# Layer 0's experts of a decoder: every expert for every row, against blocks of rows sorted by expert

## Chip, core and metric

The kernel runs on one core of one Trainium2 chip, as one program with one launch. The metric is the device time of an execution in microseconds (us). The kernel before has a median of 3429.14 us in three runs, which lie between 3427.95 and 3429.79 us.

## What is computed

The input x has 32 sequences of 100 tokens and 256 features (3200 rows), and there is a context of 361 rows for each sequence. Two layers follow each other. Each consists of a self-attention, a cross-attention on the context, and a feed-forward part with eight experts. The change is in layer 0's feed-forward part:

```
x1 = layer_norm(x + attention(x)) * ln1_w + ln1_b
gates = softmax(x1 @ gate_w.T + gate_b)             # 8 experts
_, top_idx = top_k(gates, 2)
expert_outputs = einsum('bsd,efd->bsef', x1, expert_w) + expert_b
moe_out = sum over the two chosen e of gates[e] * expert_outputs[e]
out = layer_norm(x1 + moe_out) * ln2_w + ln2_b      # then x = x + out
```

Each row needs two of eight 256x256 matrices. All arithmetic is in fp32.

## The kernel before

The 32 sequences are worked through in eight groups of four (NG = 8, G = 4, so a group has GT = 400 rows). A function `heads_attention` makes the self-attention with one loop over sequences; one turn of it is called a step here. The order of TensorE, VectorE, ScalarE and GpSimd in the loop is the order in which the program writes the calls (`in_order`). In each step the scores of the next sequence are made (line L363), masked and reduced to a maximum on VectorE (L372, L383), lowered by it on GpSimd (L384) and put through the exponential on ScalarE (L389). The weights of the present sequence are turned (L396, L401) and multiplied with the values (L412), and the sequence before is divided (L425, L432), turned (L438) and multiplied with the output matrix (the product with `f_wo`, in line L225 of the helper `project`). At four places of each step the loop calls `fill(s, part)`, which puts other work between.

In layer 0's feed-forward part `fill` holds the gating and the experts of groups that the attention has already left. `rows_of` adds the output bias on GpSimd (L1235) and normalises the rows; `gating` turns them, makes the gate logits and the two largest gates; `gates_turned` (L1293) turns the gates of a group and stores them to DRAM. From there `gate` (L1311) loads the gates of one expert, repeated over all partitions. `gated` (L1321, VectorE) multiplies the group's rows by the gates of one expert, which are zero where the expert wasn't chosen. `experts` (L1328, L1333) multiplies the gated rows of every expert with its matrix, a pair of experts in each step, after a small product that adds the biases; VectorE adds the pairs up (L1339). `end` turns the sum back (L1359), normalises it, and GpSimd multiplies, shifts and adds it to x (L1371 to L1373). After the 32 sequences the loop goes on for nine more steps, in which only the last experts, some constants and the first projections of the next self-attention (`project_group`) are left.

The next stage is layer 1's self-attention. Its loop has 16 numbers for each group: `first` (L1467) makes small products that ScalarE puts through tanh (L1473), `second` (L1486) multiplies those, and a table `around` says at which number the next group's projections stand. One of them, part 9, makes a small tile `own` on GpSimd (L1199), which part 10 multiplies on TensorE. SyncE's queue carries the DMAs; where it isn't in the set of `in_order`, a scheduler places them. In layer 1's feed-forward part, which isn't changed, rows are already sorted by expert: GpSimd sends rows with an indirect DMA (L1759), SyncE loads a place into a register and fetches a block of 128 rows from there (L2131), its matrix in the same way (L2122), and results are added into DRAM with an indirect DMA (L2352). TensorE loads the expert's number into a register after two transposes of the block (L2315).

Of the kernel before, what the change touches and what calls it, by code (L numbers as in the profile page):

```python
# [10 lines left out]
F32 = mybir.dt.float32  # L11
# [7 lines left out]
P = 128  # L19
# [47 lines left out]
def kernel(ctx: ExitStack, tc: tile.TileContext, io: dict, out: bass.AP):  # L67
# [40 lines left out]
    causal = early.tile([T, T], F32, name="causal")  # L108

# [117 lines left out]
    def in_order(more=mybir.EngineType.Pool):  # L227

        e = mybir.EngineType
        return tc.manual_schedule(engines={e.PE, e.DVE, e.Activation, more})  # L230
# [50 lines left out]
    def heads_attention(pool, w, wo, bias, norm, turn, res, fill, ready=0, over=None):  # L281
# [172 lines left out]
        with in_order():  # L454
# [17 lines left out]
            for s in range(B + 1 + fill.steps):  # L472
# [44 lines left out]
                if s == B and over:  # L517
                    over()
# [112 lines left out]
    with tc.tile_pool(name="a0", bufs=2) as pool:  # L631
# [69 lines left out]
        fill.steps = 0  # L701
# [354 lines left out]
    def top2(pool, val, n, iota8, np_=T):  # L1056
# [9 lines left out]
        for k in range(2):  # L1066
            nc.vector.tensor_tensor(
                hot[:np_, k, :n, :], bc(iota8[:np_], 1, n),
                idf[:np_, :n, k : k + 1].to_broadcast([np_, n, 8]), ALU.is_equal,
            )  # L1070
        return top, hot
# [140 lines left out]
    attn = attn_cm.__enter__()  # L1212
    with tc.tile_pool(name="f0x", bufs=1) as fixed, tc.tile_pool(name="f0", bufs=2) as pool:
        f0_we = weight(fixed, "f0_we", D, E * D)
        f0_eb = plain(fixed, "f0_eb", [E, D])
# [10 lines left out]
        x1s, x1Ts, wts, accs = {}, {}, {}, {}  # L1226

        parts = {}
        wt_dram = dram.tile([NG, E * GT], F32, name="wt_dram")

        def rows_of(g, part):

            xl = xls[g]
            if part == 0:
                nc.gpsimd.tensor_tensor(xl, xl, bc(row("f0_bo"), 1, G), ALU.add)  # L1235
            elif part == 1:
                parts[g] = stats(xl, G, tag="r", shift=True)
            else:
                x1 = pool.tile([T, G, D], F32, tag="x1", name="x1")
                scaled(x1, xl, G, parts[g])  # L1240
                x1s[g] = x1
                xls.pop(g)

        def gating(g, part):
            if part == 0:
                x1T = pool.tile([P, 2, GT], F32, tag="x1T", name="x1T")
                transposed(x1T, x1s.pop(g), "f0_ln1w", "f0_ln1b", tiles=mm_tile)
                x1Ts[g] = x1T
                return
            if part == 1:  # L1250
                x1T = x1Ts[g]
# [25 lines left out]
            lg = parts.pop(g)  # L1277
            sm = small.tile([T, G], F32, tag="smg", name="smg")
            nc.vector.tensor_reduce(sm, lg, AX.X, ALU.add)
            nc.vector.reciprocal(sm, sm)  # L1280
            gt = small.tile([T, G, E], F32, tag="gt", name="gt")
            nc.vector.tensor_tensor(gt, lg, bc(sm, 2, E), ALU.mult)
            _, hot = top2(pool, gt, G, row("iota", P))
            wt = small.tile([T, G, E], F32, tag="wt", name="wt")
            nc.vector.tensor_tensor(wt, hot[:T, 0], hot[:T, 1], ALU.add)
            nc.vector.tensor_tensor(wt, wt, gt, ALU.mult)
            wts[g] = [wt]

        def gates_turned(g):
            wt = wts[g][0]  # L1290
            pw = mm_tile()
            for i in range(G):
                nc.tensor.matmul(  # L1293
                    pw[:E, i * T : (i + 1) * T], wt[:, i, :], ident[:T, :T],
                    start=True, stop=True,
                )
            wtT = small.tile([E, GT], F32, tag="wtT", name="wtT", bufs=2)
            evac(wtT, pw[:E, :GT])
            nc.sync.dma_start(wt_dram[g].rearrange("(e t) -> e t", e=E), wtT)
            wts[g] = wtT  # L1300

        wbs, xgs = {}, {}

        def gate(n):

            if n < E * NG:
                g, e = n // E, n % E
                wb = pool.tile([P, GT], F32, tag="wb", name="wb", bufs=3)  # L1310
                nc.sync.dma_start(  # L1311
                    wb, wt_dram[g : g + 1, e * GT : (e + 1) * GT].to_broadcast([P, GT])
                )
                wbs[n] = wb

        def gated(n):
            if n < E * NG:

                tag = "xg" if n < 2 * (B - 2 * G) else ("xg", "xlT", "xrT")[(n // 2 + 1) % 3]
                xg = (pool if tag == "xg" else ahead).tile([P, 2, GT], F32, tag=tag, name="xg")  # L1320
                nc.vector.tensor_tensor(xg, x1Ts[n // E], bc(wbs.pop(n), 1, 2), ALU.mult)  # L1321
                xgs[n] = xg

        def experts(g, i, m):
            ps = mm_tile()
            at = slice(m * P, (m + 1) * P)
            if i == 0:
                nc.tensor.matmul(ps[:, :GT], f0_eb[:, at], wts[g], start=True, stop=False)  # L1328
                if m == 0:
                    accs[g] = pool.tile([P, 2, GT], F32, tag="acc", name="acc", bufs=1)  # L1330
            for e in range(2 * i, 2 * i + 2):
                for k in range(2):
                    nc.tensor.matmul(  # L1333
                        ps[:, :GT], f0_we[:, k, e * D + m * P : e * D + (m + 1) * P],
                        xgs[E * g + e][:, k, :], start=(i > 0 and e == 2 * i and k == 0),
                        stop=(e == 2 * i + 1 and k == 1),
                    )
            acc = accs[g][:, m, :]
            nc.vector.tensor_tensor(  # L1339
                acc, ps[:, :GT], x1Ts[g][:, m, :] if i == 0 else acc, ALU.add  # L1340
            )
            if m == 1:
                xgs.pop(E * g + 2 * i), xgs.pop(E * g + 2 * i + 1)

        def end(g, part):
            if part == 0:

                yo = (pool if g < NG - 1 else next_cms[0][1]).tile(
                    [T, G, D], F32, tag="x1" if g < NG - 1 else "yo", name="yo",
                    bufs=2 if g < NG - 1 else 1,  # L1350
                )
                acc = accs.pop(g)
                x1Ts.pop(g)
                for i2 in range(2):
                    pt = mm_tile()
                    for i in range(2):
                        for c in range(2):
                            tok = slice((2 * i2 + i) * T, (2 * i2 + i + 1) * T)
                            nc.tensor.transpose(  # L1359
                                pt[:T, i * D + c * P : i * D + (c + 1) * P], acc[:, c, tok], ident  # L1360
                            )
                    nc.scalar.copy(
                        yo[:, 2 * i2 : 2 * i2 + 2, :].rearrange("p g d -> p (g d)"), pt[:T, :]
                    )
                x1s[g, "end"] = yo
            elif part == 1:
# [1136 lines left out]
```

## Time and profile before

| | us |
|---|---|
| median of three runs | 3429.14 |
| the profiled execution | 3428.13 |
| its span, first to last instruction | 3426.4 |
| first product with layer 0's expert matrices (L1333) | 839.5 |
| last product with f_wo in layer 0's feed-forward part | 1189.5 |
| first product of layer 1's self-attention (L1467) | 1267.4 |
| first product of layer 1's cross-attention (x_wq) | 1609.0 |

The mean granted clock of TensorE was 0.985 of full speed. The profile counts an engine as busy from the start of an instruction to its end, and overlapping instructions once. PE is TensorE's matmuls and PEld its weight loads, DVE is VectorE, ACT is ScalarE, POOL is GpSimd, SP is SyncE; "SPq" marks an instruction of SyncE's queue. A matmul in fp32 is recorded as two instructions, a transpose as one. Each group of instructions is shown as line, engine, operation, tile written and tiles read, shapes and count, then busy us and the mean ns of one, then the idle time of its engine just before and who ended it.

### The profile page before, as it was taken

The page shows a single profiled execution, that of the slowest core. Times are in us where ns is not written, and L with a number is a line of the kernel's source. Part 1 is how long each engine was busy: PE and PEld are TensorE (multiplying, and loading weights), DVE is VectorE, ACT ScalarE, POOL GpSimd, SP SyncE. Part 2 cuts the span into 40 slices and gives each one's busy share as a digit, 9 for nine tenths or more (in the row PEclk, how much of TensorE's full clock was granted, in tenths as well). Part 3 has the DMA queues.
Part 4 walks back from the last instruction along what each step waited for, and adds up shares of the span by engine and source line. Part 5 has one row for each costly group of instructions (what it writes and reads, how often), then busy time and mean ns, then how long its engine had stood idle before and what let it go on. Part 6 is the DMA issues. An engine that isn't in the chain of part 4 may idle for free. (4 is left out here: it accounts for less than half of the span.)

```text
span 3426.4 us, 65400 instructions
## 1 busy us (share of the span) xinstructions
PE 3288.5 (96%) x25492; PEld 2217.0 (65%) x25492; DVE 1807.2 (53%) x5122; ACT 1630.8 (48%) x3597; POOL 1246.3 (36%) x936
## 2 busy tenths in 40 slices
PE   8998999989999989999999999999999989999997
PEld 6775666656666543333666666666666658899997
DVE  5776666658776658563546555564655441011111
ACT  4665666756444326665545555454555532211111
POOL 3435888854344330011323333333343332022221
PEclk8999999999999999999999999999999999999999
DMA  3002211110010120001000000000000013456665
GB/s 91 2 15 60 53 52 52 35 41 19 26 30 25 40 68 1 1 1 39 10 17 17 24 28 27 15 28 23 17 28 19 21 44 116 153 168 186 185 182 140
DMA packets 116316, 179.86 MB, mean 52 GB/s; under 512 B 16594, under 2 KB 95194, under 8 KB 115546
## 3 DMA queue, kind: packets, MB, share of 16 engines
q1 hardware_dynamic: 101340, 157.37, 14.8%
q0 software_dynamic: 12688, 15.36, 2.5%
q8 instruction: 204, 3.34, 0.4%
q10 hardware_dynamic: 1982, 2.95, 0.3%
q14 instruction: 102, 0.84, 0.1%
HBM read 150.09 MB, written 28.82 MB: 52 GB/s over the span
## 5 line engine op out<-in xcount | busy, mean ns | idle before, releaser
L1907 POOL TENSOR_TENSOR ex<-ex,rc 100x1444 f32<-100x1444 f32 x128 | 331.6, 2591 | 770.0 <-DVE rc L1906 525.8
L1898 ACT ACTIVATE ex<-s,nmx 100x361 f32<-100x361 f32 x512 | 303.2, 594 | 121.2 <-DVE nmx L1889 121.2
L384 POOL TENSOR_TENSOR s<-s,nmx 100x800 f32<-100x800 f32 x128 | 195.3, 1526 | 305.7 <-DVE nmx L383 217.7
L1473 ACT ACTIVATE h<-sc,cols 128x800 f32<-128x800 f32 x256 | 222.1, 923 | 101.4 <-PE sc L1467 99.9
L1889 DVE CUSTOM_DVE_ANT_0 s<-sc,mb 100x361 f32<-100x361 f32 x512 | 250.4, 527 | 7.5 <-PE sc L1882 7.5
L2352 POOL DMA_INDIRECT acc_dram<-y,xg x57 | 89.5, 1570 | 447.6 <-DVE y L2351 259.6
L2334 ACT ACTIVATE hgT<-sc 128x1024 f32<-128x1024 f32 x57 | 58.3, 1023 | 351.2 <-PE sc L225 351.2
L225 PE MATMUL sc<-xgT,w1b 128*128 128x128 f32 x1824 | 213.1, 275 | 0.4 <-DMA w1b<-in_f_w 0.4
L2351 DVE TENSOR_SCALAR y<-mm,gx 128x256 f32<-128x256 f32 x57 | 27.6, 484 | 347.9 <-PE mm L225 347.9
L225 PEld LDWEIGHTS sc<-xgT,w1b 128*128 128x128 f32 x1824 | 208.2, 192 | 0.7 <-issue 0.6
L225 PE MATMUL mm<-wx,hgT 128*128 x912 | 206.1, 379 | 0.0
L1333 PE MATMUL mm<-xg,f_we 128*128 128x400 f32 x512 | 191.3, 515 | 14.2 <-DVE xg L1321 13.7
L1882 PE MATMUL sc<-kT,qT 64*100 64x361 f32 x1024 | 197.6, 463 | 0.0
L1854 PE MATMUL mm<-x_wa,cT 128*128 128x512 f32 (+1 forms) x512 | 188.6, 491 | 0.2
L225 PEld LDWEIGHTS mm<-wx,hgT 128*128 128x128 f32 x912 | 169.0, 190 | 20.6
L1824 PE MATMUL mm<-cT,x_wa 128*128 128x361 f32 x512 | 179.7, 470 | 1.1 <-ACT lnT L139 1.1
L1932 PEld LDWEIGHTS mm<-eT,vb 128*64 128x64 f32 (+1 forms) x3072 | 136.6, 137 | 67.3 <-issue 66.4
L1914 PE MATMUL mm<-ident,ex 100*128 100x100 f32 (+1 forms) x1536 | 166.5, 257 | 10.1 <-ACT kT L1836 5.3
L1921 ACT COPY eT<-mm 128x400 f32<-128x400 f32 (+1 forms) x256 | 125.6, 491 | 100.2 <-PE mm L1914 99.6
L1932 PE MATMUL mm<-eT,vb 128*64 128x100 f32 (+1 forms) x3072 | 161.9, 254 | 0.0
L1914 PEld LDWEIGHTS mm<-ident,ex 100*128 100x128 f32 (+1 forms) x1536 | 143.1, 152 | 28.7 <-ACT kT L1836 7.4
L176 POOL TENSOR_TENSOR rs<-va,neghalf 100x4 f32<-100x4 f32 (+1 forms) x95 | 94.6, 998 | 178.7 <-DVE va L172 89.5
(370 smaller groups left out, 7064.7 us busy)
## 6 DMA issues: line engine op xcount, KB each, us to landing
w1b<-in_f_w SPq DMA_DIRECT2D x57, 1024.0 KB
wb<-wt_dram SPq DMA_DIRECT2D x64, 200.0 KB
cT<-in_ctxT SPq DMA_DIRECT2D x64, 180.5 KB
cT<-in_ctxT SPq DMA_DIRECT2D x128, 90.2 KB
wx<-in_f_w SPq DMA_DIRECT2D x8, 1024.0 KB
xg<-sorted_dram SPq DMA_DIRECT2D x57, 132.5 KB
cb<-in_ctx SPq DMA_DIRECT2D x32, 192.0 KB
x_dram<-x SPq DMA_DIRECT2D x32, 100.0 KB
```

The source lines that it names most:

```text
L225: nc.tensor.matmul(ps, lhsT[k], rhs[k], start=(k == 0), stop=(k == n - 1))
L384: nc.gpsimd.tensor_tensor(sm, sm, bc(nmx, 2, T), ALU.add)
L1333: nc.tensor.matmul(ps[:, :GT], f0_we[:, k, e * D + m * P : e * D + (m + 1) * P], xgs[E * g + e][:, k, :], start=(i > 0 and e == 2 * i and ...
L1473: nc.scalar.activation(h1, both[r2][:, :, :GT], AF.Tanh, bias=col("a1_b1", o))
L1824: nc.tensor.matmul(kTs[u][c][:, :S2], x1_wa[:, m * P : (m + 1) * P], cT[:, 0, :], start=True, stop=False,)
L1854: nc.tensor.matmul(ps[e][:kn, :n], cT[:, 0, at], x1_wa[:, 1024 + c0 : 1024 + c0 + n], start=True, stop=False,)
L1882: nc.tensor.matmul(ps[:T, e, :S2], qT[p0 : p0 + 64, m, tok], kT[p0 : p0 + 64, c, :], start=True, stop=True,)
L1889: nc.vector.tensor_tensor_reduce(s[:, e, :], ps[:T, e, :S2], mb, 1.0, 3.4e38, ALU.add, ALU.min, nmx[:, e : e + 1],)
L1898: nc.scalar.activation(ex[:, 2 * c + e, :], s[:, e, :], AF.Exp, bias=nmx[:, e : e + 1], scale=-1.0, accum_out=sm[:, 2 * c + e : 2 * c + e ...
L1907: nc.gpsimd.tensor_tensor(ex, ex, bc(rc, 2, S2), ALU.mult)
L1914: nc.tensor.transpose(pt[:kn, j * T : (j + 1) * T], ex[:, j, k0 : k0 + kn], ident[:T, :T])
L1932: nc.tensor.matmul(po[64 * e : 64 * e + 64, m * T : (m + 1) * T], vb[k][:kn, v0 + 64 * h : v0 + 64 * h + 64] if k < 2 else vb[2 + u % 2][: ...
```

## The change

Layer 0's experts are no longer multiplied for every row. The first four groups and the last four each get a list in DRAM, in which the rows are sorted by expert. The changes are these:

- `gating` makes for each row and each of its two experts the place in the list, from counts that two small products with a triangular matrix give. `gates_turned`, `gate`, `gated`, `experts` and `end` go.
- `send0` writes the normalised rows of a sequence to both places with two indirect DMAs on GpSimd. A small memset stands before each. `rest` fills the block behind the end of each expert's rows with zeros, and 14 stores fill spare blocks at the start. `table` makes on VectorE which expert and which place each block of 128 rows has.
- The layer norm's gain and shift and the experts' biases are folded into the matrices (`expert_bias`, `expert_weights`), in the first eight steps. The normalised rows themselves are also stored, in order, for the later sum.
- The attention loop ends with its 33rd step. Then a loop over 64 blocks (MOST = 32 in each list) follows: fetch the block, turn it, multiply it with one matrix, store the result in DRAM. SyncE's and GpSimd's order is the program's here too. Group 7's gating, the lists of the second half, group 0 and 1's endings and the first projections of the next stage stand in this loop.
- The end of a group is now: load the stored rows, apply gain and shift on GpSimd, gather the two results of each row with two indirect DMAs a sequence, add them weighed on VectorE, normalise, scale on ScalarE, multiply, shift and add. For groups 2 to 7 this stands in the loop of layer 1's self-attention (`later`).
- The bias of the attention's output is added for one sequence at a time, and the statistics of a group are made in two halves.

The core of the diff:

```diff
+    SOME, MOST = -(-2 * PART // P), (2 * PART + E * 127) // P
+    EMPTY = MOST - SOME
...
+    def rows_back(g):
+        rt = next_cms[1][1].tile([T, G, D], F32, tag="rt", name="rt")
+        nc.sync.dma_start(rt.rearrange("p g d -> p (g d)"), x1_dram[g])
+        x1back[g] = rt
+    def rows_affine(g):
+        rt = x1back[g]
+        for k, op in enumerate((ALU.mult, ALU.add)):
+            nc.gpsimd.tensor_tensor(rt, rt, bc(constants["ln1"][:, k, :], 1, G), op)
+    def outputs_back(g, i):
+        yb = next_cms[1][1].tile([T, 2, D], F32, tag="yb", name="yb", bufs=4)
+        for k in range(2):
+            nc.gpsimd.indirect_dma_start(
+                yb[:, k, :], None, y_dram[g // HALF][:, :],
+                bass.IndirectOffsetOnAxis(ap=from0[:, k, g * G + i : g * G + i + 1], axis=0),
+            )
+        ysback[g, i] = yb
+    def weighed(g, i):
+        yb = ysback.pop((g, i))
+        xi = x1back[g][:, i, :]
+        for k in range(2):
+            nc.vector.scalar_tensor_tensor(
+                xi, yb[:, k, :], gates0[:, g * G + i, k : k + 1], xi, ALU.mult, ALU.add
+            )
+    def second_norm(g, half_):
+        last_sums[g] = stats(
+            x1back[g], G, tag="e", shift=True, half=half_, got=last_sums.get(g)
+        )
+    def second_scaled(g):
+        scaled(x1back[g], x1back[g], G, last_sums.pop(g))
+    def second_added(g, engine, two=slice(0, G)):
+        rt, n = x1back[g][:, two], two.stop - two.start
+        engine.tensor_tensor(rt, rt, bc(row("f0_ln2w"), 1, n), ALU.mult)
+        engine.tensor_tensor(rt, rt, bc(row("f0_ln2b"), 1, n), ALU.add)
+        engine.tensor_tensor(xs[g][:, two], xs[g][:, two], rt, ALU.add)
...
+        for p in range(2):
+            for t in range(EMPTY):
+                at = E * RGP + t * P
+                nc.sync.dma_start(rows_dram[p][at : at + P, :], zero)
...
+        def expert_bias(e):
+            eb = biases[e] = pool.tile([P, D], F32, tag="xg", name="eb", bufs=6)
+            nc.sync.dma_start(eb, io["f0_eb"][e : e + 1].to_broadcast([P, D]))
+        def expert_weights(e, part):
+            eb = biases[e]
+            if part == 0:
+                ps = mm_tile()
+                project(
+                    ps[:, :D], [shift[:, c, :] for c in range(2)], [we[:, c, e, :] for c in range(2)]
+                )
+                nc.vector.scalar_tensor_tensor(
+                    eb, eb, 1.0 / D, ps[:, :D], ALU.mult, ALU.add
+                )
+                return
+            gain = cols[:, COL_AT["f0_ln1w"][0] : COL_AT["f0_ln1w"][1]]
+            nc.gpsimd.tensor_tensor(we[:, :, e, :], we[:, :, e, :], bc(gain, 2, D), ALU.mult)
+            nc.gpsimd.tensor_tensor(we[:, :, e, :], we[:, :, e, :], bc(eb, 1, 2), ALU.add)
+            biases.pop(e)
...
+        def send0(g, i):
+            b = g * G + i
+            for k in range(2):
+                nc.gpsimd.memset(pace, 0.0)
+                unordered(
+                    nc.gpsimd.indirect_dma_start(
+                        rows_dram[g // HALF][:, :],
+                        bass.IndirectOffsetOnAxis(ap=pos0[:, k, b : b + 1], axis=0),
+                        x1s[g][:, i, :], None,
+                    ), f"puts{g // HALF}", puts[g // HALF],
+                )
+            if i == G - 1:
+                x1s.pop(g)
...
+        def rest(p, e):
+            at = nc.sync.value_load(rest0[p][0:1, e : e + 1], min_val=0, max_val=E * RGP - P)
+            unordered(
+                nc.sync.dma_start(rows_dram[p][bass.ds(at, P), :], zero), f"puts{p}", puts[p]
+            )
...
+        def fetch(n):
+            if n >= 2 * MOST:
+                return
+            p, t = n // MOST, n % MOST
+            at = nc.sync.value_load(
+                rows_at[p][0:1, t : t + 1], min_val=0, max_val=E * RGP + (EMPTY - 1) * P
+            )
+            xg = xgs[n] = pool.tile([P, D], F32, tag="xg", name="xg", bufs=6)
+            after(nc.sync.dma_start(xg, rows_dram[p][bass.ds(at, P), :]), puts[p])
+        def turned0(n):
+            if n >= 2 * MOST:
+                return
+            p, t = n // MOST, n % MOST
+            xg = xgs.pop(n)
+            pt = mm_tile()
+            for c in range(2):
+                nc.tensor.transpose(
+                    pt[:, c * P : (c + 1) * P], xg[:, c * P : (c + 1) * P], ident
+                )
+            xT = pool.tile([P, 2, P], F32, tag="xgT", name="xgT")
+            nc.vector.tensor_scalar_add(
+                xT.rearrange("p c t -> p (c t)"), pt[:, : 2 * P], 1.0
+            )
+            xgTs[n] = xT
+            experts_[n] = nc.tensor.value_load(
+                expert_of[p][0:1, t : t + 1], min_val=0, max_val=E - 1
+            )
+        def product(n):
+            xT, e = xgTs.pop(n), experts_.pop(n)
+            po = mm_tile()
+            project(
+                po[:, :D], [xT[:, c, :] for c in range(2)],
+                [we[:, c, bass.ds(e, 1), :] for c in range(2)],
+            )
+            y = pool.tile([P, D], F32, tag="y", name="y", bufs=3)
+            nc.scalar.copy(y, po[:, :D])
+            nc.sync.dma_start(y_dram[n // MOST][n % MOST * P : n % MOST * P + P, :], y)
...
+        def after_group(g, at):
+            return {
+                3: ((output_bias, G * g + 3),), 4: ((rows_of, g, 1),), 6: ((rows_of, g, 2),),
+                8: ((gating, g, 0),), 9: ((gating, g, 1),), 10: ((gating, g, 2),),
+                11: ((gating, g, 3),), 13: ((gating, g, 4),), 14: ((gating, g, 5),),
+                15: ((send0, g, 0),), 19: ((send0, g, 1),), 23: ((send0, g, 2),),
+                27: ((send0, g, 3),),
+            }.get(at, ())
...
+        with in_order(pool_, sp_):
+            g = NG - 1
+            todo = {
+                0: ((send0, g - 1, 2), (rows_of, g, 1), (send0, g - 1, 3)), 3: ((rows_of, g, 2),), 5: ((gating, g, 0),),
+                6: ((gating, g, 1),), 8: ((gating, g, 2),), 9: ((gating, g, 3),),
+                11: ((gating, g, 4),), 12: ((gating, g, 5),),
+                13: (*((send0, g, i) for i in range(G)), (table, 1, 0)),
+                14: (*((rest, 1, e) for e in range(E)), (table, 1, 1)), 15: ((table, 1, 2),), 17: ((table, 1, 3), (table, 1, 4)),
+                16: ((make_constants, 0),), 18: ((make_constants, 1),), 20: ((make_constants, 2),),
+                21: ((rows_back, 0), (rows_affine, 0)), 23: ((rows_back, 1), (rows_affine, 1)),
+                MOST + 1: tuple((outputs_back, 0, i) for i in range(G)),
+                MOST + 5: ((weighed, 0, 0),), MOST + 7: ((weighed, 0, 1),),
+                MOST + 8: ((second_norm, 0, 0),),
+                MOST + 9: ((weighed, 0, 2),), MOST + 10: ((weighed, 0, 3),),
+                MOST + 11: ((second_norm, 0, 1), (outputs_back, 1, 0), (outputs_back, 1, 1)),
+                MOST + 14: ((second_scaled, 0),),
+                MOST + 15: ((second_added, 0, nc.vector, slice(0, 2)), (outputs_back, 1, 2)),
+                MOST + 16: ((second_added, 0, nc.vector, slice(2, 4)), (outputs_back, 1, 3)),
+                MOST + 17: ((project_group, 0, 0),), MOST + 18: ((weighed, 1, 0),),
+                MOST + 20: ((project_group, 0, 1),),
+                MOST + 21: ((weighed, 1, 1), (project_group, 0, 2)),
+                MOST + 22: ((project_group, 0, 3),), MOST + 23: ((weighed, 1, 2),),
+                MOST + 24: ((project_group, 0, 4), (weighed, 1, 3)),
+                MOST + 25: ((project_group, 0, 5), (second_norm, 1, 0)),
+                MOST + 26: ((project_group, 0, 6),),
+                MOST + 27: ((project_group, 0, 7), (second_norm, 1, 1)),
+                MOST + 28: ((project_group, 0, 8),),
+                MOST + 29: ((project_group, 0, 9), (second_scaled, 1)),
+                MOST + 30: ((project_group, 0, 10), (second_added, 1, nc.gpsimd)),
+            }
+            for n in range(4):
+                fetch(n)
+            turned0(0)
+            for n in range(2 * MOST):
+                fetch(n + 4)
+                turned0(n + 1)
+                product(n)
+                for f, *args in todo.get(n, ()):
+                    f(*args)
...
+    later = {
+        0: ((rows_back,), (outputs_back, 0), (outputs_back, 1)), 2: ((rows_affine,),),
+        3: ((outputs_back, 2),), 4: ((outputs_back, 3),), 5: ((weighed, 0),), 6: ((weighed, 1),),
+        7: ((second_norm, 0),), 8: ((weighed, 2),), 9: ((weighed, 3),), 10: ((second_norm, 1),),
+        12: ((second_scaled,),), 13: ((second_added, nc.gpsimd),),
+    }
```

## Prediction

> **What bounds the kernel now.** I read the page first, for which engine is full.
>
> ```profile
> PE 3288.5 (96%) x25492; PEld 2217.0 (65%) x25492; DVE 1807.2 (53%) x5122; ACT 1630.8 (48%) x3597; POOL 1246.3 (36%) x936
> PE   8998999989999989999999999999999989999997
> ```
>
> TensorE is the bound in nearly every slice, so work taken from it counts wherever nothing else becomes the limit. The changed stage starts near 745 us. The groups of instructions between 740 and 1300 us (busy us, mean ns, idle before) price what goes and what moves:
>
> ```profile
> L1333 PE MATMUL mm<-xg,f_we 128*128 128x400 f32 x512 | 191.3, 515 | 14.2 <-DVE xg L1321 13.7
> L384 POOL TENSOR_TENSOR s<-s,nmx 100x800 f32<-100x800 f32 x64 | 97.4, 1522 | 171.7 <-DVE nmx L383 158.8 <-ACT eT L401 12.8
> L1372 POOL TENSOR_TENSOR yo<-yo,rows 100x1024 f32<-100x1024 f32 x8 | 19.5, 2437 | 0.6
> L1328 PE MATMUL mm<-wtT,f_eb 8*128 8x400 f32 x32 | 14.9, 545 | 0.9 <-DVE acc L1339 0.9
> L1359 PE MATMUL mm<-ident,acc 128*100 128x128 f32 x64 | 8.5, 274 | 0.6 <-DVE acc L1339 0.6
> ```
>
> Busy time divided by count is the rate of TensorE, since its matmuls overlap: 191.3/512 = 374 ns for 400 columns, 8.5/64 = 133 ns for a transpose. Then the busy time by stretches: the attention loop with no expert in it yet, with experts, the tail after it, and the next layer's attention (two rows).
>
> ```profile
> 792.00:833.00 41.00, 35.69 (x445) 26.52 (x434) 32.55 (x82) 25.88 (x52) 17.74 (x22) 0.96 0.05 17
> 833.00:1189.00 356.00, 336.67 (x2835) 221.66 (x2836) 256.89 (x588) 158.11 (x313) 146.46 (x143) 1.00 0.11 30
> 1189.00:1267.00 78.00, 67.50 (x232) 38.10 (x230) 47.12 (x122) 13.82 (x27) 24.19 (x15) 0.96 0.11 31
> 1267.00:1350.00 83.00, 74.35 (x601) 28.58 (x602) 60.83 (x188) 54.69 (x66) 13.19 (x10) 0.96 0.15 48
> 1350.00:1600.00 250.00, 244.08 (x2268) 95.49 (x2266) 147.86 (x349) 169.72 (x196) 23.10 (x19) 1.00 0.01 1
> ```
>
> The columns are PE, PEld, DVE, ACT, POOL busy, clock, DMA share, GB/s. The step marks come from TensorE's timeline: each sequence ends in a product with f_wo, and the next layer starts with L1467.
>
> ```profile
> 792.31 1.11 PE L225 MATMUL mm<-f_wo,oT 128*100 128x256 f32 x4
> ...
> 832.87 1.11 PE L225 MATMUL mm<-f_wo,oT 128*100 128x256 f32 x4
> ...
> 1189.47 1.03 PE L225 MATMUL mm<-f_wo,oT 128*100 128x256 f32 x4
> ...
> 1267.39 1.61 PE L1467 MATMUL sc<-qk,a_w 32*128 32x400 f32 x12 [0.73 <-ACT yo L1362]
> ```
>
> Four steps without experts but with a whole group's gating took 832.87 - 792.31 = 40.6 us, 10.14 a step. The 24 steps with experts took 1189.47 - 832.87 = 356.6 us, 14.86 a step. The tail took 77.9 us.
>
> **1. The attention loop loses the experts.** TensorE loses 191.3 + 14.9 + 8.5 and the turned gates (64 instructions, 6.8 us): 221.5 us. The stretch 792 to 833 is the loop as it will be, so I price its step at 10.14 and add what is new. TensorE gets three rank products for each group (six small instructions at some 0.19 us, the row of the 8x8 transposes), about what the turned gates give back. VectorE gets some 14 small operations a group at 0.19 us, 0.65 us a step, beside (41 - 32.55)/4 = 2.1 us of idle time. GpSimd gets two sends a step (one scatter of 100 rows each); layer 1 has the same scatter:
>
> ```profile
> 2847.26 0.99 POOL L1759 DMA_INDIRECT sorted_dram<-x,pos  x1 [0.30 <-issue]
> 2848.55 0.99 POOL L1759 DMA_INDIRECT sorted_dram<-x,pos  x1 [0.30 <-issue]
> ```
>
> With a 0.1 us memset ahead of each that is 2.8 us a step. GpSimd is idle (41 - 17.74)/4 = 5.8 us a step, and the sends stand after both L384 of their step, when L384 of the next still waits for its maximum. So they hide; uncovered they would cost 24 x 2.8 = 67 us, since the exponentials wait for L384. I take 0.16 us a step for all of it: 10.3. The last four steps have no projections or norm left for a next group (16 instructions of 378 ns and 1.9 us of transposes a group): 8.4. New: 20 x 10.3 + 4 x 8.4 = 239.6, against 356.6: **-117**. The first eight steps get the folding of biases: 32 instructions of 128x256, at 206.1/912 = 226 ns (the wx row of the page) 7 us, and a wait for the first broadcast bias behind 14 zero stores of 128 KB, about 2 us: **+9**. GpSimd's two products an expert have its idle time there too.
>
> **2. The blocks: 64 in a row after the loop.** TensorE needs 2 x 133 + 4 x 226 = 1.17 us a block. That is not what sets the pace. Each fetch is a register load and an issue on SyncE's queue, and each result another issue; layer 1's fetches, free of waits, show the price:
>
> ```profile
> 2977.85 0.35 SPq L2131 DMA_DIRECT2D xg<-sorted_dram  x1
> 2978.98 0.37 SPq L2122 DMA_DIRECT2D w1b<-in_f_w  x1
> 2980.14 0.35 SPq L2131 DMA_DIRECT2D xg<-sorted_dram  x1
> ```
>
> 1.15 us from start to start, and 0.41 for a store (0.36 and a gap): 1.56 us a block. The store waits for ScalarE's copy of that block, and the next fetch is queued behind it. So there is a ring: fetch 1.15, landing (bounds: 2.8, the scatters of layer 1, and 3.8, its accumulating scatters), transposes and register load on TensorE, product 0.9, copy 0.37 (between the 0.33 and 0.49 of ScalarE's copies of 200 and 400 columns), store 0.41. The register load is seen once where TensorE had nothing queued:
>
> ```profile
> 2992.28 0.38 PE L2315 MATMUL mm<-ident,xg 128*128 128x128 f32 x2
> ...
> 2993.13 0.43 PE L2315 MATMUL mm<-ident,xg 128*128 128x128 f32 x2 [0.46 <-issue]
> ```
>
> 0.85 us from one pair to the next. Together 6.5 to 7.5 us, four blocks in flight: 1.62 to 1.87 a block. I take 1.75, 64 x 1.75 = 112. Ends: 1.17 (TensorE alone, if queues run ahead) and 6.5 (one block at a time).
>
> "TensorE: Matmul & The Clock Gate" of the Trainium skill, HAM oscillation, speaks against such a loop: short bursts between waits for DMA cost half the clock once an idle window of some 3.4 us is crossed. Here the granted clock was 0.59 from 761 to 764 us, just after a wait for ScalarE. By the rule gaps of 0.5 us keep the clock full; were it halved, the loop would become 64 x 2.3 = 150 us.
>
> On SyncE stand also eight zero-block stores with a register load each (8 x 1.16 = 9 us, nothing hides them as SyncE sets the pace) and some 11 weight and row loads of the next stages (5 us). Group 7's gating and the next layer's first projections (13 us of TensorE) lie in the ring's gaps; for VectorE waiting on the first gathers I take 5 us. 131 us against 77.9: **+53**. The same ends apply to what is queued there, 0 to 19 us.
>
> **3. The end of layer 0 moves into the next layer's loop** (six groups). GpSimd gets 8 gathers (no gather of rows in this trace; bounds 0.99 and the 1.57 of L2352; I take 1.3 with the gap, 10 us a group), two affine steps and three adds of 2.4 us: 22 us of an idle 38 in 41. VectorE gets 6 us a group; in the rows above it is 73% full while groups 0 and 1 are rotated, then 59%. ScalarE gets four scalings, 2.4 us, ahead of a tanh that TensorE's three buffers wait for: about 0.8 us a group. The small product "own" (L1199) is now queued on GpSimd behind three adds (7.2 us from step 12.9 of 16, at 2.6 us a step), and TensorE asks for its result in step 15: some 1.6 us a group. At the start VectorE waits for group 1's last add, 3 us. 6 x 2.4 + 3 = **+18**; ends 0 (gaps of GpSimd and VectorE absorb all) and 45 (the 7.2 us late every time).
>
> **Sum.** -117 + 9 + 53 + 18 = -37. The profiled execution took 3428.13 us (span 3426.4 and 1.7 around it), which gives 3391; the median of the three runs is 1.0 us above it: **3392 us**.
>
> **Rivals.** (a) *The ring collapses*, and it is slower: if each store keeps the next fetch back so that two blocks are in flight, a block costs 6.5/2 = 3.25 us, 96 us more: 3488. It decides from 1.75 + 37/64 = 2.33 us a block on. For it: the store and the next fetch share a queue. Against: four fetches go ahead, and y has three buffers. (b) *TensorE sets the pace of the blocks*: 1.3 us a block, SyncE's extras hidden, nothing lost in the next layer: -29 - 14 - 18, 3331. For it: layer 1's blocks hide the same register load wholly (busy 400 of 400 us from 3000 on). Against: SyncE's 1.56. (c) *The attention step doesn't fall to 10.3*: sends or gating reach L384 and the step stays at 11.8, 24 x 1.5 = 36 us back: 3428, no change. For it: TensorE lost 5.3 of 41 us in 792 to 833, waiting for VectorE's "o" behind gating.
>
> **How the numbers follow.** Forecast 0.60, (a) 0.13, (b) 0.15, (c) 0.12. The forecast's own bounds are the block at 1.57 to 1.87 (-12, +8), the extras (-19), the next layer (-18, +27) and the step at 10.0 to 11.0 (-7, +17): 3350 to 3430 if not all fall alike. The range reaches to (b) and past (c), 3335 to 3440, and leaves out most of (a). A measurement tells 0.2% (7 us) from no change. Faster: 0.95 of the forecast, (b), a fifth of (c): 0.74; same: half of (c) and a little of the forecast: 0.09; slower 0.17.
>
> **What would show it.** Steps of 10.3 us between f_wo products; some 64 fetches 1.75 us apart, SyncE never idle long; L1467 first at about 1212 us; 18 us more from there to the first product with x_wq (1608.95 now). Wrong if the blocks come over 2.3 us apart, if L384 waits behind sends, or if the next layer loses over 45 us.

## The result, and the profile after

The changed kernel is slower by 0.9 per cent: 3459.88 us in the median of four runs (3454.23 to 3464.15), against 3428.89 us of the kernel before beside it: ratio 1.0089, 95% interval 1.0072 to 1.0107. The forecast was 3392 us, and the range ended at 3440. The profiled execution took 3461.27 us (span 3459.6). Where its stages end shows which part of the kernel gained and which lost:

| stage | before, us | forecast | after, us |
|---|---|---|---|
| first to last f_wo product (attention loop) | 420.2 | 312 | 322.2 |
| from there to the first product with a_w (blocks) | 77.9 | 131 | 156.1 |
| from there to the first product with x_wq (next layer's loop) | 341.6 | 360 | 387.1 |

Some numbers of lines have moved by one or more: L384 is L385 now, L1199 is L1198, L1467 is L1722, L1486 is L1741. The page of the kernel after, its engines and TensorE's slices with the granted clock:

```profile
PE 3234.4 (93%) x25284; PEld 2199.8 (64%) x25284; DVE 1844.7 (53%) x5307; ACT 1643.9 (48%) x3641; POOL 1439.2 (42%) x1185
PE   8998999988888677999999999999999989999997
PEclk9999999999988888999999999999999999999999
```

TensorE is busy 54 us less, though 221 us of experts went and the blocks brought back at most 75 (64 x 1.17): its remaining matmuls ran longer (the mean of the f_wo product, from 850 to 1089 us, rose from 379 to 422 ns). The new hole is in the 10th to the 16th slice, 778 to 1384 us, and the clock is lower from the 12th to the 16th. The block loop in four windows (columns as before):

```profile
1096.00:1128.00 32.00, 25.39 (x115) 18.34 (x115) 13.82 (x64) 8.66 (x21) 9.80 (x19) 0.89 0.51 149
1128.00:1150.00 22.00, 8.15 (x25) 5.57 (x25) 9.73 (x42) 2.98 (x7) 8.16 (x15) 0.67 0.52 176
1150.00:1190.00 40.00, 30.44 (x120) 21.27 (x120) 8.55 (x24) 7.24 (x20) 15.53 (x11) 0.88 0.62 187
1190.00:1252.00 62.00, 48.87 (x194) 33.63 (x194) 34.06 (x90) 13.77 (x35) 21.31 (x21) 0.89 0.58 170
```

No engine is full. SyncE's queue in it, in the timeline (xg is a fetch, y_dram a store):

```profile
1119.09 0.34 SPq L1563 DMA_DIRECT2D xg<-rows_dram  x1
1119.53 0.38 SPq L1593 DMA_DIRECT2D y_dram<-y  x1
1120.74 0.34 SPq L1563 DMA_DIRECT2D xg<-rows_dram  x1
...
1130.46 0.34 SPq L1563 DMA_DIRECT2D xg<-rows_dram  x1
1133.21 0.33 SPq L1593 DMA_DIRECT2D y_dram<-y  x1
1135.40 10.48 SPq L1488 DMA_DIRECT2D rows_dram<-zero  x8
1146.71 0.35 SPq L1563 DMA_DIRECT2D xg<-rows_dram  x1
```

Undisturbed, a fetch follows the one before after 1.65 us, 0.44 to the store and 1.21 to the next fetch. 25 of the 58 recorded spacings are of that kind (up to 1.70); 32 lie between 1.86 and 4.31, and one is 16.25 us: the eight zero stores stand in it, and TensorE waits 9.24 us for the next rows. The mean is 2.36 us.

In the next layer's loop the two lines of VectorE that make z, in `rotated`, tell most. Their timeline, with two rotations of group 1, one undisturbed and one not:

```profile
1305.80 0.32 DVE L1775 TENSOR_SCALAR z<-z,cs 128x200 f32<-128x200 f32 x1
1306.15 0.42 DVE L1778 SCALAR_TENSOR_TENSOR z<-y,cs,z 128x200 f32<-128x200 f32 x1
...
1311.38 2.45 DVE L1775 TENSOR_SCALAR z<-z,cs 128x200 f32<-128x200 f32 x1
1313.86 2.48 DVE L1778 SCALAR_TENSOR_TENSOR z<-y,cs,z 128x200 f32<-128x200 f32 x1
1316.27 0.34 DVE L1775 TENSOR_SCALAR z<-z,cs 128x200 f32<-128x200 f32 x1
```

GpSimd in the same time has the affine steps of `rows_affine`, and TensorE waits for the norm (xn) that is queued on VectorE behind it. Later it waits for vm, from which own is made: vm is queued on VectorE behind a z operation of 2.50 us and one of 2.23, which stand beside the three adds. Two views follow, GpSimd's and TensorE's timeline:

```profile
1311.34 4.78 POOL L1263 TENSOR_TENSOR rt<-rt,ln 100x1024 f32<-100x1024 f32 x2
```

```profile
1319.76 0.93 PE L1158 MATMUL mm<-ident,xn 100*128 100x100 f32 x4 [6.00 <-DVE y L1751]
...
1360.13 3.03 PE L226 MATMUL mm<-xT,a_w 128*128 128x400 f32 x4 [4.66 <-DVE vm L1193]
```

Two products of 2.39 us on GpSimd, and one operation of VectorE lasts through each of them; when they end, it takes 0.34 us again.

### The profile page after: what moved, and what is told of

Same layout as the page of the kernel before. It is cut to its first block, busy times and chain, and to the rows that moved or that the text cites. A ratio compares the mean times of both kernels' runs of the same rounds, so it can differ in the third digit from the quotient of the medians.

```text
span 3459.6 us, 66769 instructions
## 1 busy us (share of the span) xinstructions
PE 3234.4 (93%) x25284; PEld 2199.8 (64%) x25284; DVE 1844.7 (53%) x5307; ACT 1643.9 (48%) x3641; POOL 1439.2 (42%) x1185
## 5 line engine op out<-in xcount | busy, mean ns | idle before, releaser
L385 POOL TENSOR_TENSOR s<-s,nmx 100x800 f32<-100x800 f32 x128 | 195.2, 1526 | 208.1 <-DVE nmx L384 119.8
L390 ACT ACTIVATE ex<-s 100x800 f32<-100x800 f32 x128 | 111.3, 870 | 100.2 <-POOL s L385 99.8
```

Source lines behind the costliest of these rows:

```text
L385: nc.gpsimd.tensor_tensor(sm, sm, bc(nmx, 2, T), ALU.add)
```

## The experiments

Fifteen more kernels ran, on four chips, each beside the kernel before on its own chip. The stretches come from each kernel's own profile.

| kernel | median us | ratio to before (95%) | loop | blocks | next layer |
|---|---|---|---|---|---|
| changed kernel | 3459.9 | 1.0089 (1.0072-1.0107) | 322.2 | 156.1 | 387.1 |
| no GpSimd products | 3412.6 | 0.9939 (0.9921-0.9958) | 322.1 | 149.7 | 353.5 |
| own first | 3452.7 | 1.0062 (1.0042-1.0082) | 322.3 | 143.8 | 389.9 |
| four groups early | 3432.8 | 1.0013 (1.0004-1.0023) | 322.1 | 163.6 | 358.9 |
| stores on ScalarE's queue | 3432.5 | 1.0002 (0.9989-1.0015) | 319.0 | 134.3 | 388.7 |
| zero stores spread | 3444.8 | 1.0037 (1.0023-1.0051) | 318.9 | 144.0 | 388.2 |
| both of these, four buffers | 3429.0 | 0.9999 (0.9988-1.0009) | 322.4 | 130.5 | 388.2 |
| and six ahead | 3429.3 | 1.0001 (0.9990-1.0011) | 319.3 | 130.0 | 388.5 |
| products doubled | 3487.0 | 1.0157 (1.0137-1.0178) | 322.3 | 178.0 | 393.0 |
| no sends | 3436.7 | 1.0014 (0.9998-1.0029) | 316.8 | 145.2 | 387.0 |
| no sends, no ranks | 3428.5 | 0.9994 (0.9984-1.0005) | 302.3 | 145.6 | 386.3 |
| stores and four groups | 3424.0 | 0.9988 (0.9978-0.9998) | 322.1 | 153.3 | 360.2 |
| lighter end | 3420.0 | 0.9965 (0.9952-0.9977) | 322.2 | 137.1 | 371.6 |
| lighter end, xg by ScalarE | 3412.9 | 0.9947 (0.9930-0.9964) | 319.5 | 135.3 | 366.9 |
| then affine steps moved | 3428.3 | 0.9989 (0.9980-0.9999) | 322.2 | 135.8 | 375.8 |
| then products on VectorE | 3418.3 | 0.9956 (0.9939-0.9973) | 322.3 | 140.4 | 365.6 |

The changed kernel, the one without products and the one with own first have the same block loop: it took 156.1, 149.7 and 143.8 us. A difference of less than some 12 us in that column says little by itself. In kernels that leave those stages alone the loop repeats within 4 us, and the next layer within 7 (386.3 to 393.0).

### The next layer's loop

**No GpSimd products.** In `later`, `2: ((rows_affine,),)` and `13: ((second_added, nc.gpsimd),)` are left out.

> Leaves out GpSimd's five products per group (two of rows_affine, three of second_added) of groups 2 to 7 in the next layer's loop, so layer 0's end is not added for these groups; gathers, weighing, sums and scaling stay. Theory A: while such a product runs, VectorE's operations that read and write only SBUF stand still until it ends (0.32 us became 2.45 at 1311 us). Then the z lines fall back from 0.60 and 0.68 us to 0.32 and 0.43, xn from 0.76 to 0.41, and the stretch from the first product with a_w to the first with x_wq falls from 387 us to 345 to 355. Rival B, the terms of the prediction (VectorE's added work, and own queued behind three adds, 1.6 us a group): the means stay as they are and the stretch falls by at most 10 us, to 377.

The stretch fell to 353.5 us, by 33.6, and the means went back. VectorE's groups from 1150 to 1650 us, of the changed kernel and then of this one:

```profile
L1751 DVE TENSOR_SCALAR y<-mm,b2h 128x400 f32<-128x400 f32 x64 | 40.2, 627 | 21.7 <-PE mm L1741 20.1 <-PE sc L1722 1.2
L186 DVE TENSOR_SCALAR xn<-x,mv,rs 100x256 f32<-100x256 f32 x32 | 22.4, 761 | 1.1 <-POOL rs L177 1.1
L1778 DVE SCALAR_TENSOR_TENSOR z<-y,cs,z 128x200 f32<-128x200 f32 x32 | 21.8, 682 | 1.1
L1775 DVE TENSOR_SCALAR z<-z,cs 128x200 f32<-128x200 f32 x32 | 19.1, 596 | 0.6
```

```profile
L1751 DVE TENSOR_SCALAR y<-mm,b2h 128x400 f32<-128x400 f32 x64 | 40.2, 627 | 21.3 <-PE mm L1741 20.9
L1778 DVE SCALAR_TENSOR_TENSOR z<-y,cs,z 128x200 f32<-128x200 f32 x32 | 13.6, 426 | 1.1
L186 DVE TENSOR_SCALAR xn<-x,mv,rs 100x256 f32<-100x256 f32 x32 | 11.4, 419 | 1.2 <-POOL rs L177 1.1
L1775 DVE TENSOR_SCALAR z<-z,cs 128x200 f32<-128x200 f32 x32 | 10.4, 324 | 0.6
```

The xn line and the two z lines lose 63.3 - 35.4 = 27.9 us of VectorE's time; L1751, which reads PSUM, stays as it was. TensorE's waits for xn fall from 17.1 to 3.3 us in this loop, those for vm from 8.7 to 0.3, and the granted clock rises from 0.93 to 0.97. Theory A holds, B falls: GpSimd's products cost through VectorE. What stays of the end's work (gathers, weighing, sums, scaling) costs 353.5 - 341.6 = 11.9 us.

**Own first.** The three adds are issued behind `around[13]`, and so behind own, instead of ahead of it:

```diff
-        12: ((second_scaled,),), 13: ((second_added, nc.gpsimd),),
+        12: ((second_scaled,),),
...
                     if 0 <= g + back < NG and not (f is rotated and (g + back, *args) not in ys):
                         f(g + back, *args)
+                if at == 13 and g + 2 < NG:
+                    second_added(g + 2, nc.gpsimd)
```

> Only the order on GpSimd is changed: own's product is issued ahead of the group's three adds. The prediction's price of own behind the adds: 1.6 us a group, so the next layer's loop falls from 387 us by about 10. Rival (the adds cost by stopping VectorE, not by own's place): it falls by less than 3 us, and the VectorE means of z and xn stay.

389.9 us, not shorter. The rival has the time right, but the means don't stay: z falls a little (682 to 615 and 596 to 538 ns), and xn, beside which the adds now fall, rises from 761:

```profile
L186 DVE TENSOR_SCALAR xn<-x,mv,rs 100x256 f32<-100x256 f32 x32 | 27.7, 928 | 9.4 <-POOL rs L177 9.4
```

TensorE's waits for vm fall from 8.7 to 0.3 us, and those for xn rise from 17.1 to 31.0 us. In the changed kernel no wait of TensorE ends at own, so its place in the queue shows no cost, though the forecast had put half of its price there; what the order of the adds decides is which operation of VectorE they stop.

**Four groups early.** All of the end of groups 2 and 3 goes into the block loop (`rt` with four buffers), and `later` works from the third group on: `if 2 <= g < NG - 2`.

> Layer 0's end for groups 2 and 3 too is made in the block loop, where VectorE and GpSimd are half idle; the next layer's loop begins with groups 4 and 5's in its third group, when nothing is rotated any more. Theory A (GpSimd's products stop VectorE's SBUF operations, and it costs most where VectorE rotates groups 0 and 1): the stretch from the first product with a_w to the first with x_wq falls from 387 us to 350 to 362, that of the blocks grows by at most 10; in all 3425 to 3440. Rival B: the work costs the same wherever it stands: the blocks grow by 20 us or more, in all 3450 or above.

358.9 us, 28.2 less; the blocks 163.6; in all 3432.8, which is theory A. So most of the 45.5 us of loss comes from the ends of groups 2 and 3, with ten of the thirty products, beside the rotations of groups 0 and 1. Their gathers and weighing moved too, so this run alone doesn't put it on the products.

### The block loop

**Stores on ScalarE's queue.**

```diff
-            nc.sync.dma_start(y_dram[n // MOST][n % MOST * P : n % MOST * P + P, :], y)
+            nc.scalar.dma_start(y_dram[n // MOST][n % MOST * P : n % MOST * P + P, :], y)
```

> Each block's result is sent from ScalarE's queue instead of SyncE's, nothing else. Theory A: SyncE's queue sets the pace of the blocks (1.2 us a fetch and 0.44 a store, 1.64 seen). Then fetches come 1.2 to 1.3 us apart and the stretch from the last product with f_wo to the first with a_w falls from 156 us to 120 to 135. Rival B: the landing of the fetched rows or TensorE at its lower clock sets it: the stretch falls by less than 8 us.

134.3 us, 10 to 22 less than the three kernels with the old loop. Theory A, at the end of its range. In the view of waits of this kernel, 1093 to 1227 us, ScalarE now waits for a free y (total, times, longest):

```profile
ACT y L1592 <- DMA y_dram<-y: 30.0, 19, 4.3
```

**Zero stores spread.** `todo[14]` loses its eight `rest`, and `todo[14 + e]` gets one each.

> The eight zero stores of the second list, one after each of blocks 14 to 21 instead of all after block 14. Theory A: their price is the queue's time alone (8 x 1.3 us, 10.5 seen), whatever their place: the stretch of the blocks falls by less than 3 us. Rival B: the burst empties the four fetches ahead, and TensorE waits for the chain to fill again (9.2 us seen at 1140): the stretch falls by 5 to 9 us.

144.0 us: within the loop's own spread, so the size stays open. The trace fits B: TensorE's longest wait for fetched rows falls from 9.2 to 3.2 us, and these waits in all from 18.2 to 10.6. The ratios (1.0037; 1.0089 in the changed kernel) speak for a gain too.

**Both, and four buffers; then six ahead.** The second kernel also has `fetch(n + 6)` with eight buffers.

> The result stores on ScalarE's queue with four buffers instead of three (with three, ScalarE waited 30 us in all for a store to land in the run with this edit alone), and the second list's zero stores spread over blocks 14 to 21. Theory A: with SyncE's queue relieved, waits for these two were what was left: the stretch of the blocks falls from 156 us to 115 to 125. Rival B: fetched rows land late while weights are loaded, whatever the queue: it stays at 128 to 135, where the store's move alone had brought it.

> As the kernel with moved stores and spread zero stores, with six blocks fetched ahead instead of four. Theory A, a ring of landing times: the stretch of the blocks falls by another 6 to 15 us below that kernel's. Rival B, TensorE's own sequence (register load, two transposes, four products, at its lower clock) sets the pace by now: within 3 us of it.

130.5 and 130.0 us. In the first, rival B by the number. Its cause isn't shown: TensorE waits 13.7 us there for VectorE's copy of the turned rows (xgT) and 7.6 us for fetched rows. In the second, B too: the ring that the prediction built its 1.75 us on isn't the limit any more.

**Products doubled.** `project` is called twice for each block.

> The changed kernel with each block's four products made twice (the second time over the first, so the result is the same): TensorE gets 64 x 4 products more, some 58 us at 226 ns. Theory A (SyncE's queue and the transfers set the pace and TensorE waits): most of it goes into its gaps, the stretch of the blocks grows from 156 us (144 to 156 in the other kernels with the same loop) by at most 20 us, and the granted clock there rises from 0.85 to over 0.92. Rival B (TensorE at its throttled clock sets the pace): it grows by 45 us or more.

178.0 us: 22 to 34 more. Between the two theories. The whole block loop, of the changed kernel and of this one:

```profile
1096.00:1252.00 156.00, 112.85 (x452) 78.81 (x452) 66.16 (x217) 32.65 (x83) 54.79 (x64) 0.86 0.57 171
```

```profile
1093.40:1271.20 177.80, 151.79 (x708) 123.12 (x708) 65.69 (x217) 32.93 (x83) 55.45 (x64) 0.92 0.49 150
```

256 products were recorded more, but TensorE is busy only 38.9 us more, while the clock rose from 0.86 to 0.92; 17 us of that went into gaps. This fits a loop without a single limit, in which the queue, the transfers and a TensorE that waits and then runs at a lower clock take turns; how much each costs wasn't told apart.

### The attention loop

**No sends; then no ranks either.** `send0` issues nothing, and `fetch` reads fixed rows of `x1_dram`; the second kernel also returns at once from parts 4 and 5 of `gating`.

> Leaves out all scatters of rows by GpSimd, in the attention loop and behind it; the blocks read 128 rows at a fixed place of x1 in place of their list's rows, so the result is another. Theory A: the sends (2.8 us a step on GpSimd) hold back the bias additions and the maxima's subtraction behind them: the step of the attention loop falls from 10.97 us to 10.3, the loop by 15 to 20 us. Rival B: gating's added work on VectorE and TensorE costs it: the step stays at 10.7 or above, the loop falls by less than 8 us.

> As the kernel without sends (which left the attention step at 10.7 us), and the ranks are left out too: the sums over experts, the three products for each group and the row numbers on VectorE; the blocks read fixed rows, the gathers row 0. Theory A: the ranks' small operations on VectorE, which stretch while GpSimd works on SBUF (one of 100x32 took 0.74 us in the mean), hold up the step: it falls to 10.2 to 10.4 us between steps 8 and 27, the loop by another 6 to 10 us below 317. Rival B: the bias additions, now four small ones a group in place of one, and the gating that was there before set it: the loop stays within 3 us of 317.

316.8 us without sends, 302.3 without ranks. GpSimd's 2.8 us a step were hidden, as the prediction had them, to within 5.4 us in all (rival B). The ranks were not: 14.5 us, more than theory A's 6 to 10; that is 0.6 a step, about as much as the 0.65 that the prediction had laid into VectorE's idle time. A line of the changed kernel's loop (800 to 1090 us) shows a part of it:

```profile
L1466 DVE TENSOR_TENSOR hot<-hot,at 100x32 f32<-100x32 f32 x12 | 8.9, 741 | 0.0
```

I had counted 0.19 us for such an operation of 32 columns, and five of the twelve take 0.18. The other seven take 0.95 to 1.17: the one at 922.68 us ends at 923.85, as GpSimd's L385 does (922.28 to 923.80). So VectorE stands still beside GpSimd's products in this loop too. The ranks were left out as a whole, so how much of the 14.5 is this, how much VectorE's order and how much TensorE's three products wasn't told apart.

### Versions

**Stores and four groups.** The two gains together.

> The moved stores, spread zero stores and four groups' ends in the block loop together. If both theories hold and the gains add: 3461 - 30 - 30 = 3400, in 3385 to 3415, below the kernel before by 0.5 to 1.3 per cent. If GpSimd's and VectorE's added work in the faster block loop becomes its bound: 3420 to 3440.

The gains don't add: 360.2 us in the next layer, but 153.3 in the blocks instead of 130.5. From 1190 to 1225 us VectorE was busy 31.6 of 35 us and GpSimd 29.1, and TensorE's waits for VectorE's copies (xgT) in the blocks rose from 13.7 to 24.5 us.

**Lighter end.** Of groups 2 and 3 only the affine steps go into the block loop, and the last bias of groups 2 to 7 is added to the residual there:

```diff
+    def bias_added(g):
+        nc.gpsimd.tensor_tensor(xs[g], xs[g], bc(row("f0_ln2b"), 1, G), ALU.add)
```

> Stores on ScalarE's queue with four buffers, zero stores spread; the affine steps of groups 2 and 3 in the block loop, the last bias of groups 2 to 7 added to the residual there too, so that a group's end in the next layer's loop has two GpSimd products (groups 2, 3) or four (4 to 7) in place of five; the product for own goes ahead of them. Theory A (each GpSimd product stops VectorE for as long as it lasts, and own waits behind the adds): the next layer's loop falls from 387 us to 360 to 370, the blocks stay at 130 to 135; in all 3400 to 3412. Rival B: the products moved into the block loop lengthen it as the four whole groups did (by 23 us): 3420 to 3430.

371.6 and 137.1 us: 3420.0 in all, the edge of rival B's total, though each stage misses A's range by only some 2 us.

**xg by ScalarE.** In `turned0`, `nc.scalar.activation(..., AF.Identity, bias=1.0)` takes the place of `tensor_scalar_add`.

> As the version with the lighter end, and the fetched rows' transposes are copied (with their + 1) by ScalarE, which was busy 33 of 132 us in the block loop, and not by VectorE, for whose copy TensorE waited 13.7 us in all. Theory A, the copy queued behind VectorE's other work holds TensorE up: the stretch of the blocks falls by 5 to 12 us against that version. Rival B: ScalarE's slower copy (0.5 us against 0.42) and its own queue of results give it back: within 3 us.

135.3 us, within 3 us: B for the blocks. As a whole this is the fastest version that leaves no work out, 0.9947 (0.9930 to 0.9964) of the kernel before, some 18 us.

**Affine steps moved; products on VectorE.** Two ways of keeping the products of groups 4 to 7 from xn.

> As the version with the copies by ScalarE, with GpSimd's two affine steps of groups 4 to 7 at step 6 of the group before, not at step 2, where the norm's subtraction (xn) for the next projection follows on VectorE. Theory A, the stop hits xn and TensorE waits for it (2.5 us seen at 1425): xn falls from 0.81 us to under 0.55 in the mean, the next layer's loop from 367 us to 355 to 361. Rival B, another operation is stopped instead (the squares): within 3 us of 367.

> As the version with the copies by ScalarE, with the four products a group of groups 4 to 7 (affine steps, gain, residual) on VectorE instead of GpSimd. Theory A: a product costs VectorE some 1.1 us of its own instead of up to 2.4 us of standing still, and VectorE has idle time in these groups (59 per cent busy before): the next layer's loop falls from 367 us to 353 to 361. Rival B: VectorE's own 4.4 us a group cost the same: within 3 us of 367 or above.

VectorE's groups of the first and of the second of them:

```profile
L1789 DVE SCALAR_TENSOR_TENSOR z<-y,cs,z 128x200 f32<-128x200 f32 x32 | 18.6, 580 | 1.1
L186 DVE TENSOR_SCALAR xn<-x,mv,rs 100x256 f32<-100x256 f32 x32 | 11.5, 424 | 5.9 <-POOL rs L177 5.9
```

```profile
L1791 DVE SCALAR_TENSOR_TENSOR z<-y,cs,z 128x200 f32<-128x200 f32 x32 | 13.6, 426 | 1.1
L186 DVE TENSOR_SCALAR xn<-x,mv,rs 100x256 f32<-100x256 f32 x32 | 11.4, 420 | 1.6 <-POOL rs L177 1.6
```

In both, xn is back at 0.42 us (it was 0.81), as A said, and neither gains: 375.8 and 365.6 us. Moved, the steps of two groups fall beside rotations (the z mean rises from 0.49 to 0.58 us) and others beside the weighing (L1278, from 0.48 to 0.61), and the loop is 9 us longer. With the products on VectorE, TensorE's waits for xn fall from 15.3 to 4.2 us, and other waits take their place, 6.5 us of them for another result of VectorE (sum, where the version before waited 1.1). So a stop of xn is real in these later groups, but what it costs is less than theory A said.

## Why the prediction was wrong

The forecast's terms and what the profiled execution had (differences in us; the first row is the time of the last f_wo product against before):

| term | forecast | measured |
|---|---|---|
| 1. the attention loop | -108 | -93.5 |
| 2. the blocks against the tail | +53 | +78.2 |
| 3. the next layer's loop | +18 | +45.5 |
| behind it | 0 | +2.9 |
| sum | -37 | +33.1 |

**Term 3 failed by its mechanism**, and it is the largest miss, 27.5 us (its own parts, 6 x 2.4 + 3, are 17.4, which was written as 18). The step reads "GpSimd gets 8 gathers ..., two affine steps and three adds of 2.4 us: 22 us of an idle 38 in 41". The idle time was there, but the two engines aren't independent: VectorE stood still in it. Without the products 33.6 of the 45.5 us come back. The Trainium skill, "SBUF — State Buffer", section "Who interferes with whom", has the rule that I didn't weigh: VectorE and GpSimd share a pair of ports, and a VectorE operation that takes it (a `tensor_scalar` with all operands in SBUF in its fast mode, or one with two SBUF inputs while GpSimd reads SBUF) and a GpSimd instruction exclude each other for the whole instruction. The trace agrees: 0.32 us became 2.45, to the end of GpSimd's product, and L1751 and L1172, which read PSUM, kept 0.63 us in both kernels. One L1751 lies inside GpSimd's product of 1351.56 to 1353.94 us and took 0.63; so does a shuffle of z behind it, which has one input in SBUF, and took 0.38 as elsewhere. For the 1.6 us a group of own no run shows a price (own first). The 11.9 us that remain without products lie between my 2.4 us x 6 and nothing.

**Term 2 was mis-sized by 13 to 25 us**: 143.8 to 156.1 us in the three kernels with this loop, for 131. The cost of one fetch and store on the queue was nearly right (1.65 us for 1.56), and the zero stores took 10.5 us for 9. The error is the "ring" of 1.75 us as a steady price: 33 of the 58 spacings are longer, and the mean is 2.36. In the timeline some of these hold a weight load or the zero stores, or a store that waits for its result; how much each adds wasn't told apart. Stores on another queue gave 10 to 22 us back. My rival (a), a collapsed ring, had the sign and this place; its point of decision was 2.33 us a block, the mean was 2.36, but it priced 96 us for it, with two blocks in flight throughout, while 25 of the spacings are still at most 1.70 us.

On the clock I had weighed "TensorE: Matmul & The Clock Gate", HAM oscillation: by the rule, gaps of 0.5 us keep the clock full. The trace doesn't bear that out. In windows of 1 us over the block loop the granted clock is 1.00 or 0.50, and between them only where it changes; it is at 0.50 for some 44 of the 156 us, and TensorE is busy in 34 of these. It drops in the waits of 4.09 and 9.24 us, as the rule has it. But it also drops about 1 us after waits of 2.12, 1.62 and 2.60 us have ended (at 1165, 1189 and 1237 us), and at 1098 and 1217 us behind several waits of which none is over 0.95 us. On the other side it stays full from 1105 to 1131 us through waits of 1.22 and 1.25 us. The four products of a block took some 2.05 us at 0.50 and 1.10 at full clock, so the 1.17 us of TensorE a block held only where the clock was full. What a full clock alone would have given wasn't measured apart; the doubled products raise it, and lengthen the loop.

**Term 1 was off by 14.5 us.** The 24 steps took 250.3 us (1096.03 - 845.69) for 239.6; the first eight grew by 8.2 for the 9 of the folding; the loop began 4.6 us later, but its start lies between 767.9 and 774.7 us in kernels with the same code ahead of it. The step "VectorE gets some 14 small operations a group at 0.19 us, 0.65 us a step", beside 2.1 us of idle time, failed: without the ranks the loop is 14.5 us shorter, so the idle time in the sum of a stage didn't cover them. Whether VectorE or TensorE's three products carry it stays open. The clock is part of it too: it was 0.91 in these 24 steps, and 0.96 in the stretch from 792 to 833 us that priced them. The sends and the folding were priced nearly right.

Of the signs that the prediction named, L1722 came first at 1252 us for 1212, the blocks' mean spacing of 2.36 us is over the 2.3 that it called wrong, and the next layer lost 45.5 us, just over the 45.

## What to carry to other kernels

Work laid into an engine's idle time is free only if nothing that it shares with a busy engine is on the path. Look for VectorE operations like those of z and xn, with their operands in SBUF, beside long GpSimd products, and lay such products where VectorE reads PSUM or waits. A chain of loads and stores in one queue kept the queue's own pace here in 25 of 58 spacings; giving the stores another queue helped. The 93.5 us gained in the attention loop were lost in the two stages behind it (78.2 and 45.5 us), where the profile before had shown idle time on VectorE and GpSimd.

## What the runs showed of the hardware that was unexpected

- GpSimd's product of 100x1024 stretched VectorE's two operations on z from 0.32 and 0.42 us to 2.45 and 2.48, each to about the end of the product. It seems to go the other way too: in the attention loop of the changed kernel GpSimd's bias addition (L1372 there) took 0.73 us at 912.99 us and 2.37 at 925.00, though its shape is the same. Beside the second, VectorE runs three products with both inputs in SBUF (L747, L749) without a gap, from 924.84 to 926.79 us; leaving them out wasn't tried.
- In a wait of 2.44 us in the attention loop (it ended at 928.37 us) the granted clock fell to 0.50 and stayed there for some 6 us.
- A gather of 100 rows of 1 KB costs GpSimd 1.02 us in the median (1.01 to 1.43) and 0.30 to the next; a scatter 0.99 (0.98 to 1.71).
- A fetch whose address doesn't come from the register followed the one before after 1.46 us where nothing disturbed it (1.65 with it), in the kernel without sends, with the register load still there.
